# Four heads to a value product in layer 1, and a new order of the drain

## The chip, the cores and the metric

The kernel runs on one core of a Trainium2 chip. The metric is the device time of one launch in microseconds (us). A core has TensorE (matrix products; in the profile PE, with its loads of the stationary operand apart as PEld), VectorE (DVE), ScalarE (ACT), GpSimd (POOL) and the queue of SyncE (SP), which issues transfers. Each works through its own list of instructions; semaphores order them between engines. Products land in PSUM, which this program uses as eight banks of 128 partitions by 512 fp32 numbers. Everything else lives in SBUF.

## The reference

Sixty-four sequences of 32 tokens with 256 features go through two layers. Each layer is attention and a feed-forward part, both added to the residual x, and each part has a conditional linear map ahead of it. The parts that matter here are layer 1's attention and its feed-forward part:

```python
# layer 1, attention: 16 heads of 16 features, sequences of 32 tokens
scores = jnp.where(causal, -jnp.inf, jnp.einsum('bhqd,bhkd->bhqk', q, k) * scale)
attn = jax.nn.softmax(scores, axis=-1)
out = jnp.einsum('bhqk,bhkd->bhqd', attn, v)
x = x + (out.transpose(0, 2, 1, 3).reshape(b, s, 256) @ W_dense + b_dense)
# layer 1, feed-forward: an expert chosen by sequence, then int8-like rounding around a gated MLP
y = jnp.einsum('bsi,bio->bso', x, W[id]) + b[id]
gate, up = split(quant_dequant(y) @ quant_dequant(w_gate_up).T)      # 704 features each
x = x + quant_dequant(silu(gate) * up) @ quant_dequant(w_down).T
```

`quant_dequant` takes the largest magnitude of each token's row, divides by 127, rounds, clips and multiplies back. So no row can be rounded before it is complete.

## The kernel before

The 2048 tokens are eight chunks of 256 (eight sequences; two groups of 128 tokens, `gi`). After layer 0's attention, eight turns follow (`turn2`, L1451). Turn n carries chunk n through layer 0's feed-forward part and layer 1's linear map, chunk n-1 through layer 1's attention, and chunk n-2 through its experts and feed-forward part. At the end of turn 7, chunk 7's attention, chunk 6's and chunk 7's feed-forward parts and the last products of chunk 5 are left. `drain` (L1554) lists them.

The program has a manual schedule: each engine gets its instructions in the order in which the Python code emits them. A function such as `quant_down` emits its products for TensorE, then its addition for VectorE, and then its store for SP, so the order of the calls fixes the order on all engines at once. PSUM banks come from one pool of eight and are handed out in rotation; a product that starts on a bank waits until the last reader of its former content is done. Most SBUF tiles used here have one buffer (`bufs=1`): `y`, `y3T`, `h3T`, `res`, `aoT`. The tiles `h` and `sg2` have two, and so has `sg`, the silu tile of `ffn_up`.

The pieces that the change touches or passes, in the order of a chunk:

- `queries_keys` (L1195) projects queries and keys, adds the bias, rotates them and transposes them in blocks of 32 on VectorE; `kb` gets the keys with one of two heads masked, one copy by ScalarE and one by VectorE.
- `project_values` (L1237) makes the values `vt`: tokens on partitions, 16 heads of 16 features.
- `attn_scores` (L1251) multiplies, adds the causal mask and subtracts the row's maximum; `attn_exp` (L1282) takes the exponential on ScalarE, in place; `attn_weights` (L1287) sums, inverts, multiplies and transposes on VectorE, which gives `pT` (keys on partitions).
- `attn_values` (L1298) multiplies values and weights. The stationary operand is the values of two heads of one sequence (32 tokens by 32 features), the moving operand the weights of the same two heads (32 tokens by 64 columns). The result has four blocks of 16 features by 32 tokens; the two on the diagonal are a head's own. It is called with k = 0 to 3, and after k = 3 the banks are emptied into `aoT`: ScalarE copies the columns of the first head times a mask that is 1 on that head's partitions and 0 on the other's (`head2`), and VectorE adds the columns of the second head times the other mask.
- `attn_out` (L1327) multiplies by the dense weights and adds into the chunk's `xT`; `tokens_back` (L414) turns `xT` into the residual `xq`.
- `run_experts` (L1360) multiplies by the gathered expert weights, adds the bias and rounds (`largest`, L194; `rounded`, L200, six instructions on VectorE); `turn_y` (L1386) transposes the result into `y3T`.
- `quant_up` (L1390) makes gate and up in two pairs of banks; silu on ScalarE (L1404) and the product on VectorE (L1405) give `h`. `quant_h` (L1408) rounds `h`. `turn_h` (L1415) transposes it into `h3T`.
- `quant_down` (L1428) multiplies by the down weights, adds the residual (L1443 in the drain) and stores the rows (L1444).

In the turns, `attn_values` stands between `turn_h` and `ffn_up` (L570), whose six silus and products (L582, L583) follow it on ScalarE and VectorE. Between these, one-column index copies (L431) on VectorE release gathers on GpSimd (L433).

Of the kernel before, what the change touches and what calls it, by code (L numbers as in the profile page):

```python
# [9 lines left out]
F32 = mybir.dt.float32  # L10
# [5 lines left out]
P = 128  # L16
B = 64
T = 32
# [58 lines left out]
def mk_kernel(  # L77
# [10 lines left out]
    nc = tc.nc  # L88
# [6 lines left out]
    def bank():  # L95
        return psum.tile([P, 512], F32, tag="ps", name="ps")
# [7 lines left out]
    def const(name):  # L104
        lo, hi = _CONST[name]
        return ct[:, lo:hi]
# [1130 lines left out]
    def project_values(ch):  # L1237
        c = chunks[ch]
        ps = bank()
        for gi in range(2):  # L1240
            for k in range(2):
                nc.tensor.matmul(
                    ps[:, gi * 256 : (gi + 1) * 256], lhsT=c["eT"][:, k, gi * P : (gi + 1) * P],
                    rhs=wv[:, k, :, :].rearrange("p h d -> p (h d)"), start=(k == 0), stop=(k == 1),
                )
        nc.vector.tensor_tensor(
            vt.rearrange("p g h d -> p g (h d)"), two(ps),
            bv.rearrange("p h d -> p (h d)").unsqueeze(1).to_broadcast([P, 2, D]), ADD,
        )
# [45 lines left out]
        nc.vector.transpose(pT.rearrange("p h t -> p (h t)"), c["s"].rearrange("p h j -> p (h j)"))  # L1295
        c["pT"] = pT

    def attn_values(ch, k):  # L1298


        c = chunks[ch]
        if k == 0:
            c["banks"] = [bank() for _ in range(4)]
        banks = c["banks"]
        gi, o = k // 2, k % 2
        for i in range(4):
            for b in range(4):
                r = slice(32 * b, 32 * b + 32)
                h = o * 8 + i * 2
                nc.tensor.matmul(  # L1310
                    banks[b][32 * i : 32 * i + 32, k * 64 : (k + 1) * 64],
                    lhsT=vt[r, gi, h : h + 2, :].rearrange("p h d -> p (h d)"),
                    rhs=c["pT"][r, gi * 16 + h : gi * 16 + h + 2, :].rearrange("p h t -> p (h t)"),
                    start=True, stop=True,
                )
        if k < 3:
            return
        aoT = work.tile([P, 4, 4, T], F32, tag="aoT", name="aoT", bufs=1)
        for b in range(4):
            of = banks[b][:, :256].rearrange("p (k e t) -> p k e t", k=4, e=2)  # L1320
            nc.scalar.activation(aoT[:, :, b, :], of[:, :, 0, :], AF.Copy, scale=const("head2")[:, 0:1])
            nc.vector.scalar_tensor_tensor(
                aoT[:, :, b, :], of[:, :, 1, :], const("head2")[:, 1:2], aoT[:, :, b, :], MULT, ADD
            )
        c["aoT"] = aoT

    def attn_out(ch):  # L1327
# [58 lines left out]
    def turn_y(ch, groups=(0, 1)):  # L1386
        c = chunks[ch]
        turned(lambda gi, k: c["y"][:, gi, k * P : (k + 1) * P], "", None, None, groups, c["y3T"])
# [19 lines left out]
    def quant_h(ch, gi):  # L1408
        h = chunks[ch]["h", gi]
        s = work.tile([P, 1], F32, tag="hs", name="hs")  # L1410
        r = work.tile([P, 1], F32, tag="hr", name="hr")
        largest(s, r, h)
        rounded(h, s, r)
# [14 lines left out]
    def quant_down(ch, gi):  # L1428

        c = chunks[ch]  # L1430
        apart = ch >= 5
        if gi == 0:
            c["res"] = work.tile([P, 2, D], F32, tag="res", name="res", bufs=1)
        if gi == 0 or apart:
            c["last"] = bank()
        ps, res = c["last"], c["res"]
        for k in range(6):
            nc.tensor.matmul(  # L1438
                ps[:, gi * D : (gi + 1) * D], lhsT=c["h3T"][:, gi, k, :], rhs=dnT[:, k, :],
                start=(k == 0), stop=(k == 5),  # L1440
            )
        if apart:
            nc.vector.tensor_tensor(res[:, gi, :], ps[:, gi * D : (gi + 1) * D], xq[ch][:, gi, :], ADD)  # L1443
            nc.sync.dma_start(out=out[ch * 256 + gi * P : ch * 256 + (gi + 1) * P, :], in_=res[:, gi, :])  # L1444
        elif gi == 1:
            nc.vector.tensor_tensor(res, two(ps), xq[ch], ADD)
            nc.sync.dma_start(
                out=out[ch * 256 : (ch + 1) * 256, :].rearrange("(g p) f -> p g f", p=P), in_=res
            )

    def turn2(n):  # L1451

        def on(i, f, *a):
            if 0 <= i < 8:
                f(i, *a)

        last = n == 7
        begun = n == 0

        def gu(*ks):  # L1460
            for k in ks:
                if not begun:
                    on(n, gate_up, k)

        if not begun:
            on(n, adapters_in)
        on(n - 1, queries_keys)
        if not begun:
            on(n, adapters_spread)
        on(n - 1, project_values)  # L1470
        for k in range(8):
            gu(k)
            if k == 3:
                if not begun:
                    on(n, gate_up_adapters, 0)
                on(n - 2, run_experts)
                for i in range(4):
                    on(n - 1, attn_scores, i)
            elif k == 5:
                on(n - 1, attn_exp)  # L1480
            elif k == 6:
                on(n - 2, turn_y)
        if not begun:
            on(n, gate_up_adapters, 1)
        on(n - 1, attn_weights)
        on(n - 1, fetch, 0)
        on(n - 1, fetch, 1)
        on(n - 2, quant_up, 0)
        on(n - 2, quant_h, 0)
        on(n - 1, fetch, 2)  # L1490
        on(n - 1, fetch, 3)
        on(n, down_adapters)
        on(n + 1, fetch_in, 0)
        if not last:
            on(n - 2, quant_up, 1)
            on(n - 2, quant_h, 1)
        for b in range(1, 4):
            on(n + 1, fetch_in, b)
        on(n, down)
        on(n - 2, tokens_back)  # L1500
        on(n + 1, tokens_in)
        on(n + 1, fetch_in, 4)
        on(n - 1, fetch, 4)
        if not last:
            on(n - 2, turn_h, 0)
            on(n - 2, turn_h, 1)
        for k in range(4):
            on(n - 1, attn_values, k)
        on(n, ffn_up, 0)
        on(n + 1, fetch_in, 5)  # L1510
        on(n - 1, fetch, 5)
        on(n, ffn_up, 1)
        on(n + 1, fetch_in, 6)
        on(n - 1, fetch, 6)
        on(n, ffn_up, 2)
        on(n + 1, fetch_in, 7)
        on(n - 1, fetch, 7)
        on(n, ffn_up, 3)
        on(n + 1, fetch_out, 0)
        on(n, ffn_up, 4)  # L1520
        on(n + 1, fetch_out, 1)
        if last:
            on(n - 1, attn_out)
        on(n, ffn_up, 5)
        on(n + 1, fetch_out, 2)
        on(n - 1, fetch, 8)
        on(n - 1, fetch, 9)
        if last:
            on(n - 2, quant_up, 1)
            on(n - 2, quant_h, 1)  # L1530
            on(n - 1, run_experts)
            for b in range(8):
                fetch(7, b)
        else:
            on(n - 2, quant_down, 0)
        on(n + 1, fetch_out, 3)
        on(n + 1, fetch_out, 4)
        on(n, ffn_down)
        on(n + 1, fetch_out, 5)
        on(n + 1, fetch_out, 6)  # L1540
        on(n + 1, fetch_out, 7)
        if last:
            on(n - 2, turn_h, 0)
            on(n - 2, turn_h, 1)
        else:
            on(n - 2, quant_down, 1)
            on(n - 1, attn_out)
        on(n, linear_adapters)
        on(n + 1, fetch_down, 0)
        on(n + 1, fetch_down, 1)  # L1550
        on(n, linear)
        on(n + 1, fetch_linear)

    def drain():  # L1554

        turn_y(6)
        queries_keys(7)
        quant_down(5, 0)
        project_values(7)
        for b in range(8, 10):  # L1560
            fetch(7, b)
        for k in range(4):
            attn_scores(7, k)
        attn_exp(7)
        quant_up(6, 0)
        attn_weights(7)
        quant_up(6, 1)
        for k in range(4):
            attn_values(7, k)
        quant_h(6, 0)  # L1570
        quant_down(5, 1)
        tokens_back(6)
        attn_out(7)
        turn_h(6, 0)
        quant_down(6, 0)
        run_experts(7, (0,))
        run_experts(7, (1,))
        quant_h(6, 1)
        turn_h(6, 1)
        turn_y(7, (0,))  # L1580
        quant_down(6, 1)
        quant_up(7, 0)
        quant_h(7, 0)
        turn_y(7, (1,))
        quant_up(7, 1)
        quant_h(7, 1)
        tokens_back(7)
        for gi in range(2):
            turn_h(7, gi)
            quant_down(7, gi)  # L1590

    for n in range(8):
# [84 lines left out]
```

## Time and profile before

| | |
|---|---|
| median of 3 runs | 1453.79 us (1450.05 to 1453.99) |
| the profiled execution | 1451.43 us |
| its span, first to last instruction | 1449.7 us |
| its mean granted TensorE clock | 0.992 |
| busy: TensorE products, loads, VectorE, ScalarE, GpSimd | 1399.7, 1086.2, 829.9, 614.1, 577.2 us |
| L1310, values of layer 1 | 1024 records, 16.8 us busy |
| L1321, L1322, emptying them | 32 instructions each, 368 and 343 ns (medians) |

The profile comes from one execution. A group of the page or of its queries has a line of the kernel, an engine, an operation, the tiles written and read, the shapes, a count, the busy time, the mean length of one and the idle time ahead of it with what ended it. Two records stand for each fp32 product, and each has a record for its load. In the timeline, a bracket gives the idle time of the engine before the instruction and the instruction that released it. The chain that ended last is followed back from the last instruction, and is shown in order of time: start, length, what. The span starts at 0.

### The profile page before, as it was taken

How to read it: one execution, taken by the hardware profiler on the slowest of the kernel's cores; microseconds unless marked ns; L12 is line 12 of the kernel's file. 1: busy time of each engine (PE TensorE's matmuls, PEld its weight loads, DVE VectorE, ACT ScalarE, POOL GpSimd, SP SyncE). 2: the span in 40 equal slices, each digit the busy share in tenths (PEclk: the TensorE clock that was granted, in tenths of full speed). 3: DMA queues.
4: the chain of work that ended last, by engine and by line, in shares of the span. 5: the costliest groups of instructions: out<-in, count | busy, mean ns of one | idle time of the engine just before them, and what ended most of it. 6: DMA issues, size and time to landing. Idle time of an engine off the chain costs nothing.

```text
span 1449.7 us, 39390 instructions
## 1 busy us (share of the span) xinstructions
PE 1399.7 (97%) x16552; PEld 1086.2 (75%) x16552; DVE 829.9 (57%) x1879; ACT 614.1 (42%) x2014; POOL 577.2 (40%) x650
## 2 busy tenths in 40 slices
PE   5899999999999999999999999999999999999996
PEld 3666777776767677767777788888887878788874
DVE  1566686867677776766565323363636262635554
ACT  1355665656575756565655512130312121212121
POOL 3423367777533333333445141524251606060320
PEclk9999999999999999999999999999999999999999
DMA  6201001321221000100001161313131304040220
GB/s 172 61 2 67 5 16 20 77 47 33 35 66 36 23 6 15 38 12 1 13 14 44 38 115 52 98 49 92 39 102 34 107 17 123 6 116 23 67 74 15
DMA packets 101625, 71.41 MB, mean 49 GB/s; under 512 B 71429, under 2 KB 88965, under 8 KB 101449
## 3 DMA queue, kind: packets, MB, share of 16 engines
q0 software_dynamic: 15744, 38.03, 9.5%
q1 hardware_dynamic: 82504, 26.34, 7.6%
q10 hardware_dynamic: 3200, 4.52, 1.0%
q8 instruction: 131, 2.15, 0.6%
q14 instruction: 46, 0.37, 0.1%
HBM read 64.54 MB, written 6.29 MB: 49 GB/s over the span
## 4 chain that ended last, share of the span: by engine, by line
PE 91%; DMA 3%; SPq 2%; DVE 2%; issue 1%; ACT 1%; POOL 0%; ACTq 0%; DVEq 0%
PE ps L779 16%; PE ps L810 15%; PE ps L1047 8%; PE ps L507 8%; PE ps L1398 5%; PE ps L578 4%; PE ps L553 3%; PE ps L1438 3%; PE ps L597 3%; PE ps L992 2%; PE ps L521 2%; PE ps L889 2%; PE ps L1206 2%; PE ps L1032 2%; SPq L276 1%; PE ps L967 1%
## 5 line engine op out<-in xcount | busy, mean ns | idle before, releaser
L433 POOL DMA_INDIRECT we<-in_ew,at x64 | 61.1, 955 | 277.5 <-DVE h L1405 203.7
L1001 ACT ACTIVATE sq<-ps 128x128 f32<-128x128 f32 x256 | 71.1, 278 | 211.6 <-PE ps L992 204.4
L793 POOL TENSOR_TENSOR qT<-ra,rb 128x256 f32<-128x256 f32 x64 | 46.6, 728 | 272.6 <-DVE rb L791 272.5
L1047 PE MATMUL ps<-wo,ogT 128*128 128x256 f32 x512 | 120.6, 389 | 6.1 <-DVE aT L896 6.1
L779 PE MATMUL ps<-hsT,wq 128*128 128x256 f32 x512 | 126.4, 390 | 0.0
L779 PE MATMUL ps<-hsT,wk 128*128 128x256 f32 x512 | 122.2, 382 | 0.0
L790 DVE TENSOR_TENSOR ra<-ps,ct 128x512 f32<-128x512 f32 x128 | 87.4, 683 | 49.9 <-PE ps L779 44.9
L810 PE MATMUL ps<-wv,hsT 128*128 128x512 f32 x256 | 115.2, 593 | 0.0
L810 PE MATMUL ps<-wg,hsT 128*128 128x512 f32 x256 | 115.1, 592 | 0.0
L1047 PEld LDWEIGHTS ps<-wo,ogT 128*128 128x128 f32 x512 | 95.8, 192 | 20.9 <-DVE aT L896 6.6
L779 PEld LDWEIGHTS ps<-hsT,wq 128*128 128x128 f32 x512 | 95.5, 192 | 18.3 <-issue 5.8
L873 DVE RECIPROCAL enz<-ps 128x256 f32<-128x256 f32 x64 | 107.5, 1721 | 2.7 <-PE ps L864 2.7
L779 PEld LDWEIGHTS ps<-hsT,wk 128*128 128x128 f32 x512 | 98.3, 192 | 13.7
L1010 POOL TENSOR_TENSOR f<-f,mhalf 128x8 f32<-128x8 f32 x32 | 53.1, 1660 | 133.5 <-DVE f L1008 133.5
L810 PEld LDWEIGHTS ps<-wg,hsT 128*128 128x128 f32 x256 | 48.6, 190 | 61.2 <-issue 54.3
L791 DVE TENSOR_TENSOR rb<-ps,ct 128x512 f32<-128x512 f32 x128 | 87.0, 680 | 0.0
L927 ACT ACTIVATE qv<-ok,nmx 128x64 f32<-128x64 f32 x256 | 85.0, 336 | 1.3 <-DVE nmx L923 1.3
L810 PEld LDWEIGHTS ps<-wv,hsT 128*128 128x128 f32 x256 | 48.6, 190 | 47.6 <-issue 45.9
L1398 PE MATMUL ps<-guT,y3T 128*128 128x352 f32 x256 | 79.5, 464 | 0.5 <-ACT y3T L395 0.5
L529 DVE TENSOR_TENSOR hT<-ps,sg 128x256 f32<-128x256 f32 x64 | 24.2, 419 | 96.9 <-ACT sg L528 96.9
L896 DVE SCALAR_TENSOR_TENSOR aT<-ps,ct 128x256 f32<-128x256 f32 x64 | 24.1, 419 | 85.6 <-PE ps L889 85.6
L433 POOL DMA_INDIRECT ag<-alora,at x56 | 53.4, 954 | 49.3 <-DVE at L431 39.3
(233 smaller groups left out, 3056.4 us busy)
## 6 DMA issues: line engine op xcount, KB each, us to landing
x<-in_x SPq DMA_DIRECT2D x8, 256.0 KB
wq<-in_wqT SPq DMA_DIRECT2D x16, 128.0 KB
wk<-in_wkT SPq DMA_DIRECT2D x16, 128.0 KB
wv<-in_wvT SPq DMA_DIRECT2D x4, 512.0 KB
wg<-in_wgT SPq DMA_DIRECT2D x4, 512.0 KB
wo<-in_woT SPq DMA_DIRECT2D x4, 512.0 KB
row<-in_wgu ACTq DMA_DIRECT2D x11, 128.0 KB
out<-res SPq DMA_DIRECT2D x5, 256.0 KB
```

The source lines that it names most:

```text
L433: nc.gpsimd.indirect_dma_start(out=to, out_offset=None, in_=table, in_offset=bass.IndirectOffsetOnAxis(ap=at, axis=0))
L507: nc.tensor.matmul(ps[:, i * 256 : (i + 1) * 256], lhsT=mlp[name, k // 4][:, j, part], rhs=c["xT"][:, j, :], start=(i == 0 and j == 0), st ...
L578: nc.tensor.matmul(ps[:, i * 256 : (i + 1) * 256], lhsT=wt[:, j, k * P : (k + 1) * P], rhs=yT[:, j, :], start=(j == 0), stop=(j == 1),)
L779: nc.tensor.matmul(ps[:, half * 256 : (half + 1) * 256], lhsT=wt[:, c, half * 256 + pr * P : half * 256 + (pr + 1) * P], rhs=hs[:, c, lo : ...
L790: nc.vector.tensor_tensor(by_t(a.rearrange("p h t -> p (h t)")), by_t(ps), cosb, MULT)
L791: nc.vector.tensor_tensor(by_t(b.rearrange("p h t -> p (h t)")), by_t(ps), sinb, MULT)
L810: nc.tensor.matmul(ps, lhsT=hs[:, c, lo + gi * P : lo + (gi + 1) * P], rhs=wt[:, c, :], start=(c == 0), stop=(c == 1),)
L873: nc.vector.reciprocal(t[:, e, :], banks[e][:, :256])
L927: nc.scalar.activation(qv[:, k, :], ok[:, k, :], AF.Exp, bias=nmx[:, k : k + 1], accum_out=rs[:, k : k + 1],)
L1001: nc.scalar.activation(sq, po[e][:, k * P : (k + 1) * P], AF.Square, accum_out=f[:, e * 4 + k : e * 4 + k + 1],)
L1047: nc.tensor.matmul(ps[:, gi * D : (gi + 1) * D], lhsT=s["ogT", gi][:, h, :], rhs=w[4][:, h, :], start=(h == 0), stop=(h == 3),)
L1398: nc.tensor.matmul(ps[:, :352], lhsT=c["y3T"][:, k, gi * P : (gi + 1) * P], rhs=guT[:, k, lo : lo + 352], start=(k == 0), stop=(k == 1),)
```

## The change

`attn_values` no longer has a k. It takes a number of heads per product, four by default. With four, the stationary operand has 64 columns (four heads of 16 features), the moving operand 128 columns (four heads of 32 tokens), and a result has sixteen blocks, of which the four on the diagonal are a head's own. For each bank, ScalarE copies the first head's columns times its mask, and VectorE adds the three others, each times its own, from the constant `quad`, which was there before. In the turns it is called with four heads (chunks 0 to 6), in the drain with two, which are the same products and the same emptying as before.

The list in `drain` has a new order. Chunk 6's first `quant_up` goes ahead of chunk 7's scores; `project_values` and chunk 5's first `quant_down` come after the scores. Around the quantizations, `quant_down(5, 1)` goes ahead of `quant_h(6, 0)`, `attn_out(7)` ahead of `tokens_back(6)`, `quant_down(6, 0)` behind the experts and `quant_h(6, 1)`, `turn_h(6, 1)` and `quant_down(6, 1)` further back, and chunk 7's two `turn_h` ahead of its two `quant_down`.

```diff
-    def attn_values(ch, k):
+    def attn_values(ch, heads=4):
         c = chunks[ch]
-        if k == 0:
-            c["banks"] = [bank() for _ in range(4)]
-        banks = c["banks"]
-        gi, o = k // 2, k % 2
-        for i in range(4):
-            for b in range(4):
-                r = slice(32 * b, 32 * b + 32)
-                h = o * 8 + i * 2
-                nc.tensor.matmul(
-                    banks[b][32 * i : 32 * i + 32, k * 64 : (k + 1) * 64],
-                    lhsT=vt[r, gi, h : h + 2, :].rearrange("p h d -> p (h d)"),
-                    rhs=c["pT"][r, gi * 16 + h : gi * 16 + h + 2, :].rearrange("p h t -> p (h t)"),
-                    start=True, stop=True,
-                )
-        if k < 3:
-            return
+        banks = [bank() for _ in range(4)]
+        tiles = 8 // heads
+        for gi in range(2):
+            for o in range(2):
+                for i in range(tiles):
+                    h = o * 8 + i * heads
+                    to, n = slice(i * P // tiles, (i + 1) * P // tiles), heads * T
+                    for b in range(4):
+                        r = slice(32 * b, 32 * b + 32)
+                        k = gi * 2 + o
+                        nc.tensor.matmul(
+                            banks[b][to, k * n : (k + 1) * n],
+                            lhsT=vt[r, gi, h : h + heads, :].rearrange("p h d -> p (h d)"),
+                            rhs=c["pT"][r, gi * 16 + h : gi * 16 + h + heads, :].rearrange("p h t -> p (h t)"),
+                            start=True, stop=True,
+                        )
         aoT = work.tile([P, 4, 4, T], F32, tag="aoT", name="aoT", bufs=1)
+        own = const("quad") if heads == 4 else const("head2")
         for b in range(4):
-            of = banks[b][:, :256].rearrange("p (k e t) -> p k e t", k=4, e=2)
-            nc.scalar.activation(aoT[:, :, b, :], of[:, :, 0, :], AF.Copy, scale=const("head2")[:, 0:1])
-            nc.vector.scalar_tensor_tensor(
-                aoT[:, :, b, :], of[:, :, 1, :], const("head2")[:, 1:2], aoT[:, :, b, :], MULT, ADD
-            )
+            of = banks[b][:, : 4 * heads * T].rearrange("p (k e t) -> p k e t", k=4, e=heads)
+            nc.scalar.activation(aoT[:, :, b, :], of[:, :, 0, :], AF.Copy, scale=own[:, 0:1])
+            for e in range(1, heads):
+                nc.vector.scalar_tensor_tensor(
+                    aoT[:, :, b, :], of[:, :, e, :], own[:, e : e + 1], aoT[:, :, b, :], MULT, ADD
+                )
...
-        for k in range(4):
-            on(n - 1, attn_values, k)
+        on(n - 1, attn_values)
...
         turn_y(6)
         queries_keys(7)
-        quant_down(5, 0)
-        project_values(7)
         for b in range(8, 10):
             fetch(7, b)
+        quant_up(6, 0)
         for k in range(4):
             attn_scores(7, k)
         attn_exp(7)
-        quant_up(6, 0)
+        project_values(7)
+        quant_down(5, 0)
         attn_weights(7)
         quant_up(6, 1)
-        for k in range(4):
-            attn_values(7, k)
+        attn_values(7, 2)
+        quant_down(5, 1)
         quant_h(6, 0)
-        quant_down(5, 1)
+        attn_out(7)
         tokens_back(6)
-        attn_out(7)
         turn_h(6, 0)
-        quant_down(6, 0)
         run_experts(7, (0,))
         run_experts(7, (1,))
         quant_h(6, 1)
+        quant_down(6, 0)
+        turn_y(7, (0,))
+        quant_up(7, 0)
+        turn_y(7, (1,))
         turn_h(6, 1)
-        turn_y(7, (0,))
+        quant_h(7, 0)
+        quant_up(7, 1)
         quant_down(6, 1)
-        quant_up(7, 0)
-        quant_h(7, 0)
-        turn_y(7, (1,))
-        quant_up(7, 1)
+        turn_h(7, 0)
         quant_h(7, 1)
         tokens_back(7)
+        turn_h(7, 1)
         for gi in range(2):
-            turn_h(7, gi)
             quant_down(7, gi)
```

More of the change, by code (lines that the diff above doesn't have):

```diff
@@ L1296, in attn_weights @@
         c["pT"] = pT
-    def attn_values(ch, k):
+    def attn_values(ch, heads=4):
         c = chunks[ch]
-        if k == 0:
-            c["banks"] = [bank() for _ in range(4)]
-        banks = c["banks"]
-        gi, o = k // 2, k % 2
-        for i in range(4):
-            for b in range(4):
-                r = slice(32 * b, 32 * b + 32)
-                h = o * 8 + i * 2
-                nc.tensor.matmul(
-                    banks[b][32 * i : 32 * i + 32, k * 64 : (k + 1) * 64],
-                    lhsT=vt[r, gi, h : h + 2, :].rearrange("p h d -> p (h d)"),
-                    rhs=c["pT"][r, gi * 16 + h : gi * 16 + h + 2, :].rearrange("p h t -> p (h t)"),
-                    start=True, stop=True,
-                )
-        if k < 3:
-            return
-        aoT = work.tile([P, 4, 4, T], F32, tag="aoT", name="aoT", bufs=1)
-        for b in range(4):
-            of = banks[b][:, :256].rearrange("p (k e t) -> p k e t", k=4, e=2)
-            nc.scalar.activation(aoT[:, :, b, :], of[:, :, 0, :], AF.Copy, scale=const("head2")[:, 0:1])
-            nc.vector.scalar_tensor_tensor(
-                aoT[:, :, b, :], of[:, :, 1, :], const("head2")[:, 1:2], aoT[:, :, b, :], MULT, ADD
-            )
@@ new lines, in attn_values @@
+        aoT = work.tile([P, 4, 4, T], F32, tag="aoT", name="aoT", bufs=1)
+        own = const("quad") if heads == 4 else const("head2")
+        for b in range(4):
+            of = banks[b][:, : 4 * heads * T].rearrange("p (k e t) -> p k e t", k=4, e=heads)
[3 more added lines that the diff above has]
+                    aoT[:, :, b, :], of[:, :, e, :], own[:, e : e + 1], aoT[:, :, b, :], MULT, ADD
+                )
```

## The prediction

> **What bounds the kernel.** First the busy time by stretches of the layer-1 turns and the drain, with the columns of its header: TensorE is busy 76.33 of 76.50 us in a turn and 55.47 of 70.30 us in the drain, where its mean granted clock falls to 0.93. So TensorE time saved in a turn is saved in full; in the drain the waits count.
>
> ```profile
> core 0: us, PE busy (x) PEld busy (x) DVE busy (x) ACT busy (x) POOL busy (x), PEclk, DMA share, GB/s
> 1154.00:1230.50 76.50, 76.33 (x1035) 63.95 (x1022) 36.60 (x102) 16.76 (x38) 28.24 (x31) 1.00 0.24 69
> 1379.40:1449.70 70.30, 55.47 (x605) 41.80 (x604) 36.81 (x79) 15.11 (x30) 6.61 (x7) 0.93 0.12 39
> ```
>
> Then the TensorE groups by form (rows by columns of the stationary tile, then K x moving columns). One fp32 product leaves two records. Busy time over count is the pace of a record; the mean of one includes its latency.
>
> ```profile
> L841 PE MATMUL ps<-rT,ws 17*128 17x256 f32 x128 | 24.2, 435 | 2.5 <-DMA ws<-in_ws2T 2.5
> L992 PE MATMUL ps<-v,w2T 64*64 64x128 f32 x1024 | 35.7, 278 | 0.0
> L1206 PE MATMUL ps<-wqk,eT 128*32 128x128 f32 x1024 | 29.9, 273 | 0.5
> L1262 PE MATMUL ps<-kb,qkT 32*32 32x64 f32 x1024 | 12.0, 225 | 0.0
> L1310 PE MATMUL ps<-pT,vt 32*32 32x64 f32 x1024 | 16.8, 234 | 2.8 <-DVE pT L1295 2.6
> ```
>
> L1310 is the product that changes. L1262 has its very shape at 11.7 ns a record against 16.4, so L1310 is paced by getting 256 loads and products issued, not by streaming.
>
> Then the chain of work that ended last, through the drain (start, length, what):
>
> ```profile
> 1400.08 1.26 DVE pT L1295
> 1401.47 1.91 PE ps L1310 x117
> 1403.37 3.63 PE ps L1438 x12
> ...
> 1414.22 0.44 DVE y L1378
> ...
> 1418.87 0.81 DVE hs L196
> ...
> 1421.27 0.60 DVE h L204
> 1421.86 0.14 issue
> 1422.00 1.09 PE ps L1422 x4
> ...
> 1443.49 2.87 PE ps L1438 x12
> 1446.36 0.02 issue
> 1446.39 0.42 DVE res L1443
> ```
>
> TensorE stands for the softmax until 1401.47, and for VectorE's three quantizations (1414.22 to 1421.86) until 1422.00. After both, L1438 takes 3.6 us instead of 2.9.
>
> Last the timeline after a turn's values, for VectorE:
>
> ```profile
> 1350.89 1.15 ACT L1321 ACTIVATE aoT<-ps,ct 128x128 f32<-128x128 f32 x4 [1.19 <-PE ps L1310]
> 1351.29 1.13 DVE L1322 SCALAR_TENSOR_TENSOR aoT<-ps,ct,aoT 128x128 f32<-128x128 f32 x4 [4.13 <-ACT aoT L1321]
> 1353.28 0.42 DVE L583 TENSOR_TENSOR gT<-ps,sg 128x256 f32<-128x256 f32 x1 [0.86 <-ACT sg L582]
> ```
>
> [...] waits of 2.59 and 6.98 us are followed by L1438 at 3.71 us instead of 2.86. [...]
>
> **Part 1, values of chunks 0 to 6.** From the timeline's start times, first L1310 record to the first record of the next line: 1.85, 2.16, 2.18, 2.17, 2.18, 2.19, 1.91 us for the seven chunks, together 14.63. The change issues 32 products of 64 stationary columns by 128 moving instead of 64 of 32 by 64: 64 records for 128, the same 4096 moving columns, over 8 tiles instead of 16. A lone 128x256 record paces at 216 ns (L1438, twelve in 2.59), so 128 columns stream in 107. L992 (2x2 tiles, 128 columns) starts records 26.9 ns apart, L1206 (4 column tiles) 27.0, which is 107/4; four row tiles also run together (L841: eight records of 256 columns start within 0.34 us, in two bursts of four). With eight tiles 107/8 = 13.4 ns, above the 8.4 ns steady spacing of L1262 records, hence streaming sets it: 64 x 13.4 = 0.86, plus 0.14 to the next form (L1310's own last-start-to-next), plus 0.10 for issue stalls (L1310 shows two or three of 170 to 290 ns a chunk; half the records, and I take a fraction). I take 1.10 a chunk, 7.70 in all: **-6.9 us**. Bounds: 1.00 (no stall), and 64 x 26.9 + 0.14 = 1.86 if eight tiles pace like four: -7.6 to -1.6.
>
> VectorE gets 12 masked additions a chunk for 4, ScalarE the same four. Three on a bank depend on each other: 0.343 + 0.03 each, 0.265 to the next bank's, so 1.0 us a bank and 4.0 for 1.13. Cover: L583's first product, ready 2.0 us after the first addition, waits 2.0 longer; the next come 1.73 us apart and take 0.42 plus two index copies, so the third is on time. ScalarE's third silu needs the first sg buffer (two buffers): free 4.9 us after the ACT copies begin, wanted at 5.2. The four PSUM banks come up again only after four ffn_up. Index copies behind it, and POOL's gathers, leave 2 us later for tiles used some 20 us on. Cost 0; without that cover 2.9 a chunk.
>
> **Part 2, the drain.** Chunk 7 keeps two heads a product, so its pieces keep their prices; only order changes. SP's six stores and POOL's two gathers keep their order; two VectorE index copies go with fetch, off the path. Issue prices on TensorE: queries_keys 3.63, quant_up 4.84, scores 1.50, project_values 1.73, quant_down 2.59, values 1.84, attn_out 1.73, tokens_back 0.44, turn_h 0.66, run_experts 0.93 a group, half a turn_y 0.22. On VectorE: quant_h 3.08, a group's y 2.29, softmax before exp 3.95 (from 0.46 after the scores), after it 4.15; exp 1.06. I lay them on three in-order queues from 1378.79, when turn_y(6) starts. The old order so laid out ends at 1444.54; measured 1446.81. The missing 2.3 is the half clock (L1438 twice 0.96 late, the transposes 0.9).
>
> The new order: quant_up(6,0) fills rope and transpose (its silus wait behind ScalarE's kb but are ahead of exp), scores at 1387.84. Project_values, quant_down(5,0) and quant_up(6,1), 9.16 in all, follow scores until 1398.50; the softmax, no longer behind quant_up(6,0)'s table load and products, gives pT at 1399.19. A wait of 0.69 where there were 2.9 (counted from the last issue; the profile's idle is 0.2 to 0.4 shorter). Values, quant_down(5,1), attn_out, tokens_back end 1405.79. Here a **new wait**: quant_h(6,0) now stands behind quant_down(5,1)'s residual on VectorE, which waits for that product until 1403.96. It ends 1407.47, attn_out's addition behind it 1408.35, so turn_h(6,0) waits 1.80 and run_experts 0.16. Then experts, and quant_down(6,0) covers the y of group 0: turn_y(7,0) at 1412.86 without a wait, 0.62 for the y3T copy, quant_up(7,0) covers y of group 1 and quant_h(6,1), done 1417.20. The 7.0 us hole is gone. turn_y(7,1), turn_h(6,1), quant_up(7,1), quant_down(6,1), turn_h(7,0), tokens_back end 1427.94. **Second new wait**: quant_h(7,1) stands behind quant_down(6,1)'s residual, 1427.19; turn_h(7,1) at 1430.82, a wait of 2.88. Two quant_downs and the last residual: 1437.46.
>
> Waits: 0.21 + 2.93 + 0.61 + 7.05 + 0.40 + 0.62 + 0.80 + 0.61 = 13.2 become 0.69 + 1.80 + 0.16 + 0.62 + 2.88 = 6.15: -7.1, and 1444.54 - 1437.46 = 7.1. A wait of 2.88 may or may not fill enough of a clock window (2.59 did); a window of half clock costs 1.7. I take 1.2, between 0 and two windows, 3.4. Drain: 1446.81 - (1437.46 + 1.2) = **-8.1**, from -9.3 to -5.9.
>
> **Sum.** -6.9 - 8.1 = -15.0. The profiled execution took 1451.43 (span 1449.7): 1436.4. The median shown is 2.4 above it, two of three runs being near 1453.9; I set the change against the median: **1438.8**.
>
> **Rivals.** (a) Eight tiles pace like four, 26.9 ns: only four-tile rows are seen at full streaming, and L1262 reaches 6.4-fold. Values -1.6, drain -8.1: 1444.1. (b) The drain's two new waits do most of the harm: each residual wait is followed by a clock window and softmax slips behind project_values' addition by another 2 us; drain -4, values -6.9: 1442.9. (c) Slower: the eight extra additions reach the path. The place is the third silu of ffn_up, 0.3 us from its sg buffer. If that slack isn't there and TensorE loses the additions in full, 2.9 x 7 = 20.3 against -15.0: +5.3, 1459.1. It decides from 2.1 us a chunk. Against it: TensorE meets the banks of the delayed L583 only eight allocations later, some 10 us. (d) Four-head products serialize to the price of full-array ones, 107 ns a record: 6.9 us a chunk, +33.7 - 8.1, 1479; L992 and L841 speak against it.
>
> **Chances.** Forecast 0.72, (a) 0.11, (b) 0.12, (c) 0.04, (d) 0.01. The forecast's own range is 1434 to 1442; the other faster cases carry it to 1445.5; below, the lowest run shown, 1450.05, less the two low bounds, 7.6 and 9.3, is 1433.2. A difference under 0.3%, 4.4 us, is about what a measurement of this kernel can't tell from none: faster 0.94, same 0.02, slower 0.04.
>
> **What would show it.** Values: 64 records a chunk, next line 1.0 to 1.2 us after the first, turns 75.1 us long for 76.25; at 1.9, (a). L583 at most 2.3 us later after the values and no new TensorE wait in ffn_up, else (c). Drain: no wait above 1 us for h L204 around run_experts; waits near 1.8 at turn_h(6,0) and near 2.9 at turn_h(7,1), both released by VectorE's h after L1445's residual. I am wrong if the turns don't shorten, or if the drain holds a wait that I haven't named.

## The result, and the profile after

The changed kernel takes 1435.43 us (median of 5 runs, 1433.85 to 1436.26) against 1453.37 for the kernel before (5 runs, 1450.05 to 1453.99), so the medians lie 17.9 us apart. The ratio taken over the runs is 0.9893, with a 95% interval of 0.9882 to 0.9905, which makes 15.5 us less, between 13.8 and 17.1. A later set of runs on another chip gave the same ratio, with medians 15.8 us apart; 15.5 is used below. The forecast was 15.0 less and 1438.8. The profiled execution after took 1435.43 with a span of 1433.7, against 1451.43 and 1449.7.

First the busy time by stretches of the kernel after, one turn of layer 1 and the drain; the columns are those of the header.

```profile
core 0: us, PE busy (x) PEld busy (x) DVE busy (x) ACT busy (x) POOL busy (x), PEclk, DMA share, GB/s
1148.98:1224.51 75.53, 75.46 (x951) 63.47 (x951) 39.23 (x110) 16.52 (x37) 28.35 (x31) 1.00 0.26 70
1371.37:1433.70 62.33, 54.56 (x610) 41.27 (x608) 36.73 (x79) 15.48 (x31) 6.91 (x8) 0.97 0.16 46
```

A turn is 0.75 to 0.8 us shorter than before (75.5 for 76.3), and TensorE still fills it. VectorE has 2.6 us more in it, which cost the turn nothing. In the drain TensorE does nearly the work that it did before (54.56 us for 55.47, at a granted clock of 0.97 for 0.93); what went is idle time, 14.8 us before and 7.8 now.

Then the TensorE groups by form of the kernel after: the values of chunks 0 to 6 in the first row, those of chunk 7 in the second.

```profile
L1312 PE MATMUL ps<-pT,vt 32*64 32x128 f32 x448 | 9.8, 282 | 0.0
L1312 PE MATMUL ps<-pT,vt 32*32 32x64 f32 x128 | 1.5, 225 | 0.1
```

From the timeline's start times, the first record of the values to the first of the next line takes 1.15, 1.36, 1.37, 1.37, 1.43, 1.38 and 1.29 us in the seven turns, 9.34 together for 14.63 before: **5.3 us** gone, where 6.9 was forecast.

The chain of work that ended last, through the drain of the kernel after:

```profile
1391.74 0.07 issue
1391.81 1.47 PE ps L1312 x81
1393.28 2.80 PE ps L1440 x12
...
1396.10 0.43 DVE res L1445
...
1398.92 0.60 DVE h L204
1399.52 0.04 issue
1399.57 0.66 PE ps L1424 x4
...
1416.46 2.60 PE ps L1440 x12
...
1419.09 0.42 DVE res L1445
...
1421.91 0.60 DVE h L204
1422.51 0.14 issue
1422.64 0.63 PE ps L1424 x4
1423.27 0.43 PE ps L1426 x2
1423.70 6.66 PE ps L1440 x24
1430.36 0.02 issue
1430.39 0.42 DVE res L1445
```

The values (L1312) no longer wait for the softmax, and the 7.0 us hole ahead of `turn_h` is gone. The chain leaves TensorE twice, each time in the form that was forecast: a `quant_down` (L1440), its residual on VectorE (L1445), the rounding behind it up to `h` (L204), and only then the transposes (L1424). The view of the waits, for TensorE in the drain (line waited for and its releaser; us in total, times, longest), has nothing else:

```profile
PE ps L1424 <- DVE h L204: 3.8, 2, 2.5
PE ps L1400 <- ACT y3T L395: 0.5, 1, 0.5
```

After the second wait, of 2.50 us, the granted clock is 0.50 for one window of 3.41 us from 1423.13, and the last two `quant_down` take 6.66 us. From the first record of `turn_y(6)` to the end of the last residual the drain is 59.44 us, for 68.02 before: **8.6 us** gone, where 8.1 was forecast.

Last the timeline after the values of turn 7 in the kernel after:

```profile
1342.13 1.36 PE L1312 MATMUL ps<-pT,vt 32*64 32x128 f32 x64
...
1344.01 4.22 DVE L1324 SCALAR_TENSOR_TENSOR aoT<-ps,ct,aoT 128x128 f32<-128x128 f32 x12 [3.65 <-ACT aoT L1322]
...
1348.14 0.41 DVE L583 TENSOR_TENSOR gT<-ps,sg 128x256 f32<-128x256 f32 x1
...
1348.91 0.38 ACT L582 ACTIVATE sg<-ps 128x256 f32<-128x256 f32 x1 [1.34 <-PE ps L578]
```

The twelve additions take 4.22 us (4.0 forecast). The first product of `ffn_up` (L583), whose silu was done at 1345.83, starts 2.3 us late, and the third silu comes on time: its 1.34 us of idle time end with TensorE's product, as the other silus' do.

So the two parts give 5.3 + 8.6 = 13.9 us. The two spans differ by 16.0. The other 2.1 lies in the first 100 us of the program, where nothing was changed: ScalarE's hundred-and-first instruction starts at 97.9 us before and at 95.9 after, and the distance stays about 2.2 up to layer 1. The profiled execution of before issues the first product of layer 1's attention (L1206) at 863.0 us, nine others (after and eight experiments on chips of its kind) between 859.1 and 860.9, among them one whose code is that of before up to the drain. So the 2.1 us belong to that one execution and not to the change; what made them isn't known.

### The profile page after: what moved, and what is told of

It reads as the page before. It is cut to its first block, busy times and chain, and to the rows that moved or that the text cites. A ratio compares the mean times of both kernels' runs of the same rounds, so it can differ in the third digit from the quotient of the medians.

```text
span 1433.7 us, 38539 instructions
## 1 busy us (share of the span) xinstructions
PE 1390.6 (97%) x16104; PEld 1081.1 (75%) x16104; DVE 848.1 (59%) x1935; ACT 613.5 (43%) x2014; POOL 576.5 (40%) x650
## 4 chain that ended last, share of the span: by engine, by line
PE 92%; DMA 3%; SPq 2%; DVE 1%; issue 1%; ACT 1%; POOL 0%; ACTq 0%; DVEq 0%
PE ps L779 16%; PE ps L810 15%; PE ps L1047 8%; PE ps L507 8%; PE ps L1400 5%; PE ps L578 4%; PE ps L553 3%; PE ps L1440 3%; PE ps L597 3%; PE ps L992 2%; PE ps L521 2%; PE ps L889 2%; PE ps L1206 2%; PE ps L1032 2%; SPq L276 1%; PE ps L967 1%
## 5 line engine op out<-in xcount | busy, mean ns | idle before, releaser
L1047 PEld LDWEIGHTS ps<-wo,ogT 128*128 128x128 f32 x512 | 95.9, 192 | 20.7 <-DVE aT L896 6.8
L779 PEld LDWEIGHTS ps<-hsT,wk 128*128 128x128 f32 x512 | 97.9, 191 | 13.4
```

Of the source, the lines that this page charges most:

```text
L779: nc.tensor.matmul(ps[:, half * 256 : (half + 1) * 256], lhsT=wt[:, c, half * 256 + pr * P : half * 256 + (pr + 1) * P], rhs=hs[:, c, lo : ...
L1047: nc.tensor.matmul(ps[:, gi * D : (gi + 1) * D], lhsT=s["ogT", gi][:, h, :], rhs=w[4][:, h, :], start=(h == 0), stop=(h == 3),)
```

## The experiments

Nearly all experiments edit the changed kernel; each is compared with the kernel before on its own chip. The chips are not alike: the first four kernels ran on one where the kernel before takes 1646.8 us, the others on chips where it takes 1450.6 and 1451.7, as in the comparison above.

**Four heads in the turns, the drain in its old order.** The values are as in the changed kernel, `drain` lists its calls as before.

```diff
         queries_keys(7)
+        quant_down(5, 0)
+        project_values(7)
...
         attn_values(7, 2)
-        quant_down(5, 1)
         quant_h(6, 0)
+        quant_down(5, 1)
-        attn_out(7)
         tokens_back(6)
+        attn_out(7)
...
+            turn_h(7, gi)
             quant_down(7, gi)
```

> The change's products of four heads in the turns, with the old order of the drain. Theory A (the two parts add): each turn after the first is 75.5 us long instead of 76.3, the seven chunks' values take 9.3 us instead of 14.6, and the whole is 5.3 us below before; the drain, from turn_y(6) to the last residual, is as before, 68.0 us. Theory B (part of what the turns save is given back where the turns end, so that the new drain was needed for it): the drain is longer than 68.5 us and the whole less than 4 us below before.

Measured on the first chip: 1652.01 us (1645.55 to 1655.86) against 1646.8 (1643.1 to 1653.43), ratio 1.0026 (1.0014 to 1.0039), some 4 us slower. In the trace its drain takes 76.6 us, where 68.0 was expected; 4.8 us of that is idle time of TensorE for "issue" ahead of L1206. On the other kind of chip:

> Four heads to a product in the turns, the drain in its old order. Theory: the gain is seven times the shorter stretch of the values, 14.6 - 9.3 = 5.3 us below the kernel before; turns 75.5 us, drain 68.0 as before. Rival (the four-head products gain nothing, all comes from the order): 0. Where instructions come late the values take as long in either form, and the difference goes towards 0.

Measured: 1442.72 us (1441.84 to 1446.16) against 1451.73 (1448.8 to 1453.71), ratio 0.9945 (0.9933 to 0.9958), 8.0 us less with an interval from 6.1 to 9.7.

**The new order alone.** Two heads to a product everywhere, `drain` as in the changed kernel; `attn_values` is that of before.

```diff
-        attn_values(7, 2)
+        for k in range(4):
+            attn_values(7, k)
```

> The new order of the drain alone, with two heads to a product everywhere. Theory A (the parts add): the drain takes 59.4 us as in the changed kernel, 8.6 less than before, and the whole is 8.6 us below before; turns stay at 76.3 us. Theory B: the drain's gain depends on when the turns end, so it takes over 60.5 us here. Rival (b) of the forecast (two new waits do most of the harm) would have the whole only 4 us below before.

Measured on the first chip: 1636.28 us (1632.14 to 1643.77), ratio 0.9926 (0.9899 to 0.9953). And again:

> The drain's new order, two heads to a product everywhere. Theory: 8.6 us below the kernel before, turns 76.3 as before, drain 59.4 with waits of about 1.34 and 2.50 us at the two turn_h. Rival (the parts share one gain): the whole 15.5, or less than 5. With the values alone it should add up to the changed kernel within 1.5 us.

Measured: 1440.22 us (1438.42 to 1443.62) against 1451.73, ratio 0.9927 (0.9914 to 0.9941), 10.6 us less with an interval from 8.6 to 12.5. Its waits are 1.34 and 2.50 us. Beside these two ran the changed kernel itself:

> The changed kernel unaltered, to stand beside its two halves. If the chip gives instructions at the pace of the first pair of traces: about 15.5 us below the kernel before; turns about 75.5 us, L1312 first record to next line about 1.4 us a chunk, drain 59.4 us. If instructions come late, as on the chip of the first four experiments: about 12 below, and L1312 above 4 us a chunk.

Measured: 1435.95 us (1433.88 to 1436.97), ratio 0.9893 (0.9878 to 0.9908); L1312 takes 1.21 to 1.48 us a chunk, the drain 59.44.

Both parts gain alone, so it is two gains and not one shared. But 8.0 + 10.6 = 18.6 is 3.1 more than the 15.5 of both together, and I had expected them to add up within 1.5. The three intervals reach some 2 us to either side each, so the runs alone don't show that the 3.1 is more than noise. The traces offer a reason, for one execution of each. The turns are 5.4 us shorter with the values alone and 0.4 longer with the drain alone (5.1 shorter in the kernel after). The drain is 66.60 us with the values alone, 1.4 below that of before, and 57.76 with the order alone, 1.7 below that of the changed kernel. In each the waits are the same, and one window of half clock is missing: the wait of 2.59 us for the softmax and that of 2.50 us at `turn_h(7, 1)` brought none. 1.4 + 1.7 = 3.1. The last section says when a wait brings one. The clock of the timed runs isn't seen window by window, so that this holds for their medians too is argued only.

**What paces a four-head product.** The forecast had put the eight tiles at the streaming rate. Two kernels move one size each. The first lets half the weights' columns stream: the second two heads' weights are left out of each product, and the second and third addition read the first two blocks again.

```diff
-                            banks[b][to, k * n : (k + 1) * n],
+                            banks[b][to, k * n : k * n + 2 * T],
...
-                            rhs=c["pT"][r, gi * 16 + h : gi * 16 + h + heads, :].rearrange("p h t -> p (h t)"),
+                            rhs=c["pT"][r, gi * 16 + h : gi * 16 + h + 2, :].rearrange("p h t -> p (h t)"),
...
-                    aoT[:, :, b, :], of[:, :, e, :], own[:, e : e + 1], aoT[:, :, b, :], MULT, ADD
+                    aoT[:, :, b, :], of[:, :, e % 2, :], own[:, e : e + 1], aoT[:, :, b, :], MULT, ADD
```

> The changed kernel with 64 moving columns instead of 128 in each of the turns' value products (half of the weights are left out; VectorE reads the first two blocks again), so as many instructions with half the streaming. In the changed kernel a chunk's first 32 records ran in bursts of eight every 110 ns, 13.7 ns each, and the second 32 at 18 to 20 ns with stalls. Theory Q (the second half is paced by how fast TensorE is handed loads and products [...]): the first 32 records fall to 7 to 9 ns, the second 32 stay at 17 ns or more, and where instructions come slowly they stay as slow as they were. Theory S (streaming sets both halves): both fall to about 8.4 ns and a chunk takes 0.75 us to the next line.

The second issues every four-head product twice.

```diff
-        for gi in range(2):
+        for gi in (0, 0, 1, 1) if heads == 4 else (0, 1):
```

> The changed kernel with each of the turns' value products done twice in a row, 128 records a chunk. Theory S (streaming): a chunk takes 0.86 us more than the changed kernel's 1.36, and turns grow by that. Theory Q (handing over): the added 64 records cost as the second half does, 18 to 20 ns each, so 1.15 us or more a chunk, and much more where stalls in that half are longer.

Measured, first record to next line: with half the columns 1.08 to 1.32 us in turns 2 to 7 (1.29 to 1.43 in the kernel after; turns 75.1 to 75.4 us); with twice the products 2.34 to 2.50 us in turns 1 to 7, 1.09 more a chunk on average (turns 76.44 to 76.55). One execution each: 1429.74 and 1441.69 us, beside 1450.62 for the kernel before. The groups by form, of half the columns and then of twice the products:

```profile
L1312 PE MATMUL ps<-pT,vt 32*64 32x64 f32 x448 | 7.9, 233 | 0.0
```

```profile
L1312 PE MATMUL ps<-pT,vt 32*64 32x128 f32 x896 | 17.4, 280 | 0.0
```

The busy time doesn't halve with the columns (9.8 to 7.9). The single records say more. These are the start-to-start distances in ns of the 64 records of one chunk (turn 4), of the kernel after and of half the columns:

```
after:         6 7 7 6 7 7 6 114  6 7 7 6 7 6 7 63  6 6 8 6 6 7 7 63  7 6 7 7 6 7 7 62
               7 6 7 7 16 16 50 24 17 17 16 5 12 17 1 25 17 16 16 17 16 22 16 17 16 17 15 18 9 7 172
half columns:  7 7 6 7 7 6 7 61  6 6 7 7 6 7 7 12  6 7 6 7 7 6 7 13  5 7 7 6 7 7 6 23
               58 9 16 17 17 16 17 21 16 18 16 16 17 121 28 17 10 7 16 17 17 16 4 14 3 17 17 16 17 16 226
```

The first 32 records go in bursts of eight, 487 ns in all (292 with half the columns). A burst takes 109 ns, close to the 107 that the forecast has for the 128 columns of one record: eight tiles at work together, as forecast. The second 32 go one by one, mostly 16 to 17 ns apart in both, and halving the columns doesn't shorten them: over the seven chunks they take 471 to 748 ns in the kernel after (624 on average) and 404 to 833 with half the columns (620). So streaming sets the first half and not the second. Twice the products fits: each added record costs 1.09 us / 64 = 17 ns, where streaming would cost 13.4. It also rules out another reading of the step, since record 32 is where the products go over from the first group of tokens to the second (`gi`): with twice the products the records 33 to 64 repeat the first group, and they are as slow. In the kernel before, too, the step comes at record 32 of 128, with the first group still under way.

**More additions.** Two further VectorE instructions a bank, 20 for 12 in a chunk; they take a maximum with the fourth head's block, which changes what is computed.

```diff
+            for e in range(2 if heads == 4 else 0):
+                nc.vector.scalar_tensor_tensor(
+                    aoT[:, :, b, :], of[:, :, 3, :], own[:, 3:4], aoT[:, :, b, :], MULT, MAX
+                )
```

> The changed kernel with eight more VectorE operations a chunk on the way out of the banks (a maximum with the fourth head's masked block, twice a bank, which changes what is computed), 20 for 12, so some 3.0 us more VectorE work after each chunk's values. If the additions are covered with room to spare (the forecast's zero), no wait of TensorE appears in ffn_up and turns grow by less than 0.1 us. If the slack is the 0.3 us that was worked out for the third silu and TensorE soon runs out of banks behind it (rival c), turns grow by 1 to 3 us.

Measured: 1435.57 us, turns 75.40 to 75.58 us, as in the kernel after. The timeline after the values of its turn 7 (L1338 is `attn_out`'s product there):

```profile
1343.62 8.90 PE L578 MATMUL ps<-yT,f 128*128 128x256 f32 x40
...
1350.79 0.74 DVE L1328 SCALAR_TENSOR_TENSOR aoT<-ps,ct,aoT 128x128 f32<-128x128 f32 x2
1351.44 0.41 DVE L583 TENSOR_TENSOR gT<-ps,sg 128x256 f32<-128x256 f32 x1
...
1351.95 0.78 ACT L582 ACTIVATE sg<-ps 128x256 f32<-128x256 f32 x2 [4.18 <-DVE at L431]
1352.15 1.71 PEld L1338 LDWEIGHTS ps<-aoT,dw 128*128 128x128 f32 x8
```

Here the third silu does stand for its buffer, 4.18 us idle and some 3 us late (the profile names the index copy right behind L583 on VectorE), and still TensorE's 40 records of L578 take the 8.90 us that they take in the kernel after. So rival (c) has its mechanism and not its price: the late silu doesn't reach TensorE here. The next limit can be read here too. `attn_out` loads `aoT` at 1352.15, and the last addition ends at 1351.53: 0.6 us were left, where the kernel after has 3.7.

**TensorE kept busy through the second wait.** Five products that nobody reads, of 256 columns each, go ahead of the last `turn_h`.

```diff
+        idle = bank()
+        for k in range(5):
+            nc.tensor.matmul(idle[:, :D], lhsT=dnT[:, k, :P], rhs=dnT[:, k, :], start=True, stop=True)
```

> The changed kernel with five products of 256 columns, whose result nobody reads, between the last tokens_back and the last turn_h, where TensorE waits 2.50 us. If that idle time is what brings the half clock, no window of half clock follows, and from the last turn_h's first record to the last residual it takes 6.6 us instead of 8.2. If the half clock isn't tied to the idle time, the stretch stays at 8.2 us. The wait for the rounding itself stays: turn_h starts when it did.

Measured: 1433.13 us, drain 57.70 us, no half clock in it. The chain of this kernel at its end:

```profile
1421.36 0.60 DVE h L204
1421.96 0.04 issue
1422.01 0.66 PE ps L1424 x4
1422.66 0.22 PE ps L1426 x2
1422.88 5.20 PE ps L1440 x24
```

The transposes still start when `h` is done. What follows takes 5.20 us for 6.66, and from the last `turn_h` to the last residual it is 6.5 us for 8.2: the half clock after the second wait cost 1.7 us. That it stayed away isn't chance of the kind that the last section describes: on the clock's grid of this execution one window reaches from 1418.96 to 1422.37, and a wait of 2.50 us up to 1422.01 would have lain in it whole. So idle TensorE caused the half clock.

**The two waits taken away.** `quant_h(7, 1)` goes ahead of `quant_down(6, 1)`, so that its rounding doesn't stand behind that residual; in the second kernel `quant_h(6, 0)` goes ahead of `quant_down(5, 1)` too, as it stood in the kernel before.

```diff
-        quant_down(5, 1)
         quant_h(6, 0)
+        quant_down(5, 1)
...
+        quant_h(7, 1)
         quant_down(6, 1)
         turn_h(7, 0)
-        quant_h(7, 1)
         tokens_back(7)
         turn_h(7, 1)
```

> The changed kernel with quant_h(7,1) listed ahead of quant_down(6,1), which moves six VectorE instructions ahead of one residual addition and nothing else. If the 2.50 us wait ahead of the last turn_h comes from VectorE's order, it shrinks to 0.2 to 0.5 us, the half clock that follows it goes too (1.6 us), and the drain takes 55.5 to 56.0 us instead of 59.4. If the wait came from the rounding itself being too long, it stays above 1.5 us and the time with it. If the slow clock isn't tied to this wait, only 2.2 us go.

> As the run before it, and quant_h(6,0) listed ahead of quant_down(5,1) too. The wait of 1.34 us ahead of the first turn_h goes to nearly nothing, and run_experts then waits some 0.5 us for attn_out's addition instead, so 1.1 us less than the run before it: a drain of 54.5 to 55 us. If that addition is what bounds the stretch rather than the rounding ahead of it, the gain is under 0.4 us.

Measured on the first chip: 1636.7 us (1632.43 to 1640.17), ratio 0.992 (0.9898 to 0.9943), and 1637.14 us (1633.66 to 1641.21), ratio 0.9933 (0.9909 to 0.9956). In the traces the waits are gone, first the 2.50 and then the 1.34 too, and the drain shrinks from 66.5 (the new order alone) to 64.3 and 62.8 us. The times don't tell these kernels from the new order alone (0.9926). The groups by form say what chip this is: of the new order alone there, the values of all eight chunks with two heads to a product, and of the values alone, the four-head products.

```profile
L1310 PE MATMUL ps<-pT,vt 32*32 32x64 f32 x1024 | 21.7, 247 | 17.3 <-issue 17.2
```

```profile
L1312 PE MATMUL ps<-pT,vt 32*64 32x128 f32 x448 | 21.7, 298 | 11.6 <-issue 11.4
```

On this chip TensorE stands idle without waiting for anything that the profile shows: 17.3 us ahead of the first group, 17.2 of it "issue", where before's row of L1310 has 2.8, most of it for the softmax. A chunk's values take 4.6 to 5.0 us with two heads and 4.1 to 4.4 with four (turns 2 to 6), so the smaller count of products buys 0.5 us a chunk there. Why the values alone came out slower than the kernel before isn't settled: no trace of the kernel before was taken there.

The second of the two kernels once more, on the other kind of chip:

> The changed kernel, with quant_h(6, 0) ahead of quant_down(5, 1) and quant_h(7, 1) ahead of quant_down(6, 1). Theory: both waits (1.34 and 2.50) go, and with them the half clock after the second (1.7): drain 59.4 - 3.8 - 1.7 = 53.9, some 4 to 5.5 us below the changed kernel. Rival: a later wait on VectorE takes the place of those removed, because the residuals now stand behind the rounding; then within 1.5 us of the changed kernel.

Measured: **1429.43 us** (1427.86 to 1430.73), ratio 0.9846 to the kernel before (0.9834 to 0.9859), and 6.5 us below the changed kernel beside it. Its drain by stretch (columns as in the first view), and the chain in it:

```profile
1371.03:1427.80 56.77, 52.66 (x610) 40.07 (x608) 36.66 (x79) 15.40 (x31) 6.92 (x8) 1.00 0.17 51
```

```profile
1392.93 2.79 PE ps L1440 x12
1395.72 1.73 PE ps L1334 x8
1397.45 0.44 PE ps L418 x4
1397.89 0.44 PE ps L1424 x4
...
1417.72 0.60 DVE h L204
1418.31 0.14 issue
1418.45 0.63 PE ps L1424 x4
1419.08 0.22 PE ps L1426 x2
1419.30 5.20 PE ps L1440 x24
```

The first `turn_h` (L1424 at 1397.89) now comes straight behind TensorE's own work, and the clock is full throughout. The second is still released by `h`, with 0.2 us of idle time ahead of it for 2.50. No other wait took their place: besides this one, TensorE's only wait in the drain is the 0.5 us for `y3T` that the changed kernel has too. The drain takes 53.91 us; 53.9 was expected. Of the 6.5 us by the medians the drain explains 5.5.

## Why the prediction was right, and where it was not

**Sum.** The sum was 15.0, the changed stretches give 13.9, the runs 15.5 with 13.9 just inside the interval. The time of 1438.8 came out 3.4 too high. 2.4 were added because the median of before lay above the profiled execution, and that execution, at 1451.43, itself carried 2.1 us at its start that the one after didn't have; the 1.1 us that the changed stretches gained less than forecast go the other way: 1451.43 - 13.9 - 2.1 = 1435.4. That the forecast lies within 0.5 us of the 15.5 is in part luck: its first term was 1.6 too large and its second 0.5 too small, and the runs show 1.6 more than the changed stretches do.

**Part 1, the values: right for half of the records, one term mis-sized.** Eight tiles do work side by side, which the forecast estimated from forms with four: the first 32 records take 0.49 us, 15.2 ns each, or 13.6 without the one longer gap behind the first burst. The step that failed is "hence streaming sets it: 64 x 13.4 = 0.86". It holds for these 32 records; the rest cost 0.47 to 0.75 us, mostly 20 ns each with their stalls, and 0.20 to 0.25 to the next form for the 0.14 taken. That is 1.36 for 1.10 in a typical chunk, and the sign that was set, the next line 1.0 to 1.2 us after the first record, held in one chunk of seven. It could have been read in the trace of before: there the first 32 records of a chunk's L1310 take 265 ns, and the other 95 distances 1.75 us, 18.5 ns each. A rate taken from a whole group's mean, or from another line's, hid the step at record 32.

The single records also say where the gain comes from, in us, for the chunk of turn 4 and for chunk 7 in the drain:

| | first 32 records | the others | to the next line | sum |
|---|---|---|---|---|
| turn 4 before, 128 records | 0.27 | 1.76 | 0.14 | 2.17 |
| turn 4 after, 64 records | 0.49 | 0.63 | 0.25 | 1.37 |
| chunk 7 after, 128 records of two heads | 0.24 | 1.02 | 0.14 | 1.40 |

The first 32 records became slower, because each has twice the columns. All of the gain lies behind them, where 31 distances are left of 95. In the drain of the kernel after, two heads to a product take 1.40 us already, as long as four heads in a turn; whether four heads would gain anything there wasn't run. Rival (a), 26.9 ns throughout, needed 1.86 a chunk; rival (d) is far off.

**The additions: right.** Cost 0, with the delay forecast (2.0, measured 2.3) and the third silu on time. The margin was wider than 0.3 us: with eight more additions the third silu was some 3 us late and TensorE never waited.

**Part 2, the drain: right, nearly step by step.** The three queues laid out by hand, each in the order of the list, counted from the start of `turn_y(6)`, against the trace of after:

| | forecast | measured |
|---|---|---|
| values start | 20.40 | 20.44 |
| `turn_h(6, 0)` | 28.80 | 28.20 |
| `turn_y(7, 0)` | 34.07 | 33.56 |
| `turn_h(7, 1)` | 52.03 | 51.27 |
| last residual done, half clock included | 59.87 | 59.44 |

VectorE keeps the order of the list there: chunk 6's first `h` is complete at 1381.21, and its rounding starts at 1396.44, behind the residual of 1396.10 for which VectorE stood idle 1.31 us. Of the waits, 0.69, 1.80, 0.16, 0.62 and 2.88 were forecast, counted from the last issue; the profile's idle times are 0.09, 1.34, none, 0.46 and 2.50, shorter by up to 0.6. Most of the 0.6 us gained before `turn_h(6, 0)` is chunk 7's values: 1.84 us was a price at half clock, and without the wait before them they take 1.40. It fits that in the forecast's check on the old order the half clock, twice 0.96 and 0.9, makes 2.8 and not the 2.3 that were missing: some of it was in the prices already. Rival (b), more harm from the two waits, is refuted for the whole; but the waits are where the change left the most: 5.5 us of drain, as the last experiment showed.

**Half clock.** 1.2 us was taken, between none and two windows. The profiled execution has one, at 1.7. In two other traces with the same waits (the order alone, and half the columns) there is none.

## What to carry to other kernels

When many small products go in a row, look at the single records' distances, not at a group's mean: the head of the run can go by its columns and the tail not, as here, where half the columns took 292 ns for 487 in the head and 620 for 624 in the tail. With four heads to a product the head got slower (0.49 us for 0.27 in turn 4) and the tail gave all of the gain (0.63 for 1.76), because it has a third as many records; the tiling paid in the tail by its count of products, not by its columns. When a listed order is changed, lay all in-order queues out beside each other; here that gave each new wait to within half a microsecond, and naming what stands ahead of the waiting instruction (the rounding behind a residual that waits for a product) was already the next improvement.

## What was not expected of the hardware

The step at record 32. In every turn on these chips the first 32 records of L1310, L1312 and of the scores' L1262 go at one pace, 265 ns together for L1310, 265 to 274 for L1262 and 487 for L1312, and the later ones more slowly. L1206, which starts a record only every 27 ns on its four tiles, has no step of that kind (in turn 4 of the kernel after 28.0 ns a record over the first 32, 26.6 behind them). What sets the pace behind the step is open. The prediction and theory Q put it down to the issue of loads and products; the trace of before has 5.6 us of "issue" ahead of the loads of L1310, in 15 pieces over the eight chunks, and none of the traces shows what spaces the records between these pieces. The 17 ns are no fixed price of a record or of a 64-column load: L1262's later records are 10.5 ns apart on average, those of chunk 7's two-head products in the drain, which have the form of L1310, 10.7, and with half the columns fourteen distances in a row of L1312 are 8 to 9 ns in turn 1. On the first chip the later records of L1312 are 105 to 114 ns apart on average (turns 2 to 6 of the values alone), a mean of many near 17 and of single gaps up to 1242, which begin at the step or somewhat ahead of it.

Which waits bring half clock. The prediction left open whether 2.88 us would. Half clock comes in windows of 3.41 us that lie on a fixed grid: in each of the ten traces from these chips all changes of the granted clock lie multiples of 3413 ns apart, to 3 ns. In the ten drains, idle time of 2.40 us or more within one window of the grid was always followed by a window of half clock, and 1.53 us or less never; nothing between was seen. The same wait of 2.50 us fell inside one window in four of these traces (in one of them all but 0.1 us), and straddled two in two others, and so cost 1.7 us or nothing. So in these drains an idle time of 2.40 us, well under the 3.41 of a window, was enough.
